# A state space layer: two states in one scan of 512 columns, their start values added to the scan's input

## The chip, the cores and the metric

The kernel runs on one core of a Trainium2 chip. The metric is the device time of one execution in microseconds (us). Before the change it is 8366.49 us, the median of three runs (8362.25 to 8367.0).

A core has five engines that work side by side and wait for one another through semaphores: TensorE (PE in the profile; its weight loads are PEld), VectorE (DVE), ScalarE (ACT), GpSimd (POOL) and SyncE (SP), which starts the transfers here. Each takes its own instructions in program order. SBUF is the large memory on the core, PSUM the small one that TensorE writes to.

## The reference

The program has two layers with a residual each; the change touches only the first. It is a selective state space layer over four images of 64 x 64 positions, taken as L = 4096 tokens. Cut to what matters:

```python
x_dbl = jnp.einsum('bld,ed->ble', xc, x_proj_w)          # xc: 768 channels after a convolution and SiLU
dt = x_dbl[..., :DT_RANK]                                 # 24
Bm = x_dbl[..., DT_RANK:DT_RANK + D_STATE]                # 16
Cm = x_dbl[..., DT_RANK + D_STATE:]                       # 16
dt = jax.nn.softplus(jnp.einsum('blr,dr->bld', dt, dt_w) + dt_b)
A = -jnp.exp(A_log)                                       # 768 x 16

def step(h, inp):
    dt_t, B_t, C_t, x_t = inp
    dA = jnp.exp(dt_t[:, :, None] * A[None])
    dBx = (dt_t * x_t)[:, :, None] * B_t[:, None, :]
    h = dA * h + dBx
    y_t = jnp.einsum('bdn,bn->bd', h, C_t)
    return (h, y_t)

_, ys = jax.lax.scan(step, h0, seq)                       # h0 is zero
y = jnp.moveaxis(ys, 0, 1) + xc * D
y = y * _silu(z)
out = jnp.einsum('bld,cd->blc', y, out_proj_w)
```

Each of the 768 channels has 16 states, and each state is a recurrence along the 4096 tokens: h = dA * h + dBx. The second layer (attention in windows of 7 x 7) comes after the first and is the same in both kernels.

## The kernel before

The 768 channels are six tiles of 128 partitions (ND = 6, index d). The tokens are cut into chunks of T = 256; a chunk of one image is called a step (STEPS = 4 images x 16 chunks = 64, index I). The 16 states of a channel tile are taken in groups of NG = 4 (index g), so a step has M = 24 pairs m = (d, g), each with two halves of two states. A half is a slot: 48 slots in a step. What does not belong to the scans themselves (the projections, the softplus, the output of the step before) is spread over the slots by a plan, and each engine works in the order in which the program emits its instructions.

These are the parts that the change touches. The state's scan needs three inputs: the decay da (ScalarE, into PSUM), the driving term db = dt x B, and the state with which the chunks before ended.

```python
def dt_x(I, d, h):
    h["dtx"][d] = w2.tile([P, T], F32, tag="dtx", name=f"dtx_{I}_{d}")
    nc.gpsimd.tensor_tensor(
        h["dtx"][d], h["dt"][d // 2][:, d % 2, :], h["xc"][d // 2][:, d % 2, :], ALU.mult)

def dt_x_copied(d, h):
    nc.scalar.copy(dtx_ps[:, d % 2, :], h["dtx"][d])           # into PSUM, for VectorE

def driven(I, m, h, eng):                                      # 9 of 24 on GpSimd, 15 on VectorE
    d, g = divmod(m, NS // NG)
    db = w2.tile([P, NG, T], F32, tag="db", name=f"db_{I}_{m}", bufs=6)
    dtx = dtx_ps[:, d % 2, :] if eng is nc.vector else h["dtx"][d]
    eng.tensor_tensor(db, dtx.unsqueeze(1).broadcast_to([P, NG, T]), h["B"][g], ALU.mult)
    dbs[I, m] = db

def decay(I, m, half, h):
    d, g = divmod(m, NS // NG)
    da = ps_a.tile([P, 2, T], F32, tag="da", name="da")        # one PSUM bank, of two
    for k in range(2):
        n = g * NG + 2 * half + k
        act(da[:, k, :], h["dt"][d // 2][:, d % 2, :], AF.Exp, scale=nega[:, d, n : n + 1])
    das[I, m, half] = da

def scans(I, m, half, hs):
    d, g = divmod(m, NS // NG)
    da = das.pop((I, m, half))
    for k in range(2):
        j = 2 * half + k
        n = g * NG + j
        nc.vector.tensor_tensor_scan(
            hs[:, j, :], da[:, k, :], dbs[I, m][:, j, :],
            state[:, d, n : n + 1] if I % NCHUNK else 0.0,
            ALU.mult, ALU.add)

def with_c(I, m, h, hs):
    d, g = divmod(m, NS // NG)
    nc.gpsimd.tensor_copy(state[:, d, g * NG : (g + 1) * NG], hs[:, :, T - 1])
    nc.gpsimd.tensor_tensor(hs, hs, h["C"][g], ALU.mult)

def summed(I, m, h, hs):
    ...                                # TensorE adds the four states' rows up in PSUM (y)
```

The slots in which dt x and the driving terms are made (slot, 1 = on VectorE), and the loop over all m:

```python
driven_at = (
    (-4, 0), (-1, 1), (1, 1), (2, 1), (4, 0), (7, 1), (8, 0), (10, 1),
    (12, 0), (15, 1), (17, 1), (18, 1), (20, 0), (22, 1), (24, 0), (26, 1),
    (26, 1), (26, 1), (30, 0), (33, 1), (36, 0), (39, 1), (40, 0), (43, 1),
)
dt_x_at = (-5, 2, 10, 18, 22, 34)
...
for n in range(STEPS * M):
    I, m = divmod(n, M)
    hs = w2.tile([P, NG, T], F32, tag="hs", name=f"hs_{I}_{m}", bufs=5)
    for half in range(2):
        if 2 * n + half + 1 < len(halves):
            nxt = halves[2 * n + half + 1]
            decay(*nxt, steps[nxt[0]])
        if half == 0:
            if behind:
                with_c(*behind[-1])
            ...                        # summed() of an earlier m
        scans(I, m, half, hs)
        run(I, 2 * m + half, 2 * m + half + 1)     # what the plan has for this slot
    behind.append((I, m, steps[I], hs))
```

A few instructions of the group statistics (once per image) serve as a comparison in the prediction. L251 copies three columns from PSUM, L252 to L254 work on three columns with all operands in SBUF:

```python
def deviation():
    nc.vector.tensor_copy(gm[:, :, 0], t["psmc"][:, 0:NJ])
    nc.vector.tensor_tensor(dev, mv[:, :, 0:1], gm[:, :, 0:1], ALU.subtract)
    nc.vector.tensor_tensor(dev, dev, dev, ALU.mult)
    nc.vector.tensor_tensor(dev, dev, mv[:, :, 1:2], ALU.add)
```

Of the kernel before, what the change touches and what calls it, by code (L numbers as in the profile page):

```python
# [8 lines left out]
F32 = mybir.dt.float32  # L9
# [39 lines left out]
def two_layers(  # L49
# [221 lines left out]
    def layer0(x1s, mvs, gms1):  # L271

        with ExitStack() as es:
            es.enter_context(tc.manual_schedule(engines=in_step))
            ps_a = es.enter_context(tc.tile_pool(name="ps_a", bufs=2, space=PSUM))
# [6 lines left out]
            gms, gbs, st1s = {}, {}, {}  # L282
            dtx_ps = ps_x.tile([P, 2, T], F32, name="dtx_ps")

# [45 lines left out]
            def normed(I, h, at):  # L330
# [10 lines left out]
                def by_group():  # L341
                    h["xn"] = w2.tile([P, NJ, T], F32, tag="xn", name=f"xn_{b}_{i}", bufs=1)
                    for j in range(NJ):
                        act(
                            h["xn"][:, j, :], h["x"][:, j, :], AF.Identity,
                            scale=gms[b][:, j, 1:2], bias=gbs[b][:, j, :],
                        )
# [17 lines left out]

                def root():
                    act(h["var"][:, 0, :], h["var"][:, 0, :], AF.Ln, bias=eps)
                    act(h["var"][:, 0, :], h["var"][:, 0, :], AF.Exp, scale=-0.5)

                at(12, load)  # L370
                at(22, by_group)
                at(24, lambda: mean("xn", "mu"))
                at(26, lambda: with_row("mu", ALU.subtract))
                at(30, square)
                at(31, lambda: mean("sq", "var"))
                at(34, root)
                at(35, lambda: with_row("var", ALU.mult))
# [16 lines left out]
            def with_bias(dst, pb, bias):  # L394

                for k in range(2):
                    act(dst[:, k, :], pb[:, k, :], AF.Identity, bias=bias[:, k : k + 1])

            def prepared(I, h, at):
# [22 lines left out]
                at(-11, kept)  # L422
                for p, (x, c, z) in enumerate((
                    ((-10, -9, -6), (1, 2, 5), (9, 10, 13)),
                    ((-6, -5, -2), (3, 4, 7), (12, 13, 16)),
                    ((-4, -3, 0), (7, 8, 11), (15, 16, 19)),
                )):
                    d = 2 * p
                    pair(("x", p), x, lambda pb, k, d=d: in_proj(pb, k, d + k, h["xn"]))
                    at(x[2], lambda p=p, d=d: with_bias(  # L430
                        xb[:, d : d + 2, KC - 1 :], h["pb"][("x", p)], binp[:, d : d + 2]
                    ))

                    def conv_out(p=p, d=d):
                        c = w2.tile([P, 2, T], F32, tag="xc", name=f"xc_{b}_{i}_{d}", bufs=6)
                        with_bias(c, h["pb"][("c", p)], cvb[:, d : d + 2])
                        h["xc"].append(c)

                    pair(("c", p), c, lambda pb, k, d=d: conv(pb, k, d + k))
                    at(c[2], conv_out)  # L440

                    def z_out(p=p, d=d):
                        z = w2.tile([P, 2, T], F32, tag="sz", name=f"sz_{b}_{i}_{d}", bufs=6)
                        with_bias(z, h["pb"][("z", p)], binp[:, ND + d : ND + d + 2])
                        h["sz"].append(z)

                    pair(("z", p), z, lambda pb, k, d=d: in_proj(pb, k, ND + d + k, h["xn"]))
                    at(z[2], z_out)
# [15 lines left out]
                def rows():  # L464
# [6 lines left out]
                    for tag in "BBBCBCCC":  # L471
                        g = len(h[tag])
                        t = bc.tile([P, NG, T], F32, tag=tag, name=f"{tag}_{b}_{i}_{g}")
                        r0 = g * NG + (NS if tag == "C" else 0)
                        src = rows[r0 : r0 + NG, :]
                        nc.sync.dma_start(t, src.unsqueeze(0).broadcast_to([P, NG, T]))
                        h[tag].append(t)

                at(26, burst)
                at(28, lambda: x_proj((0, 1, 2)))  # L480
                at(29, lambda: x_proj((3, 4, 5)))
                at(32, rows)

                def softplus(q, first):
# [12 lines left out]
                    def parts():  # L497
                        t["e"] = w2.tile([P, 2, T], F32, tag="sp_e", name=f"spe_{b}_{i}_{q}")
                        t["r"] = w2.tile([P, 2, T], F32, tag="sp_r", name=f"spr_{b}_{i}_{q}")
                        for k in range(2):  # L500
                            bias = dtb[:, 2 * q + k : 2 * q + k + 1]
                            act(t["e"][:, k, :], t["pb"][:, k, :], AF.Abs, bias=bias)
                            act(t["r"][:, k, :], t["pb"][:, k, :], AF.Relu, bias=bias)

                    def exped():
                        act(t["e"], t["e"], AF.Exp, scale=-1.0)
                        act(t["pb"], t["e"], AF.Identity, bias=1.0)
# [15 lines left out]
                    at(first, project)  # L523
                    at(first + 3, parts)
                    at(first + 4, exped)
                    at(first + 5, logged)
                    at(first + 6, lost)
                    at(first + 7, added)

                for q, first in enumerate((34, 36, 46)):  # L530
                    softplus(q, first)

            dbs, das = {}, {}
# [21 lines left out]
            def decay(I, m, half, h):  # L555

                d, g = divmod(m, NS // NG)
                da = ps_a.tile([P, 2, T], F32, tag="da", name="da")
                for k in range(2):
                    n = g * NG + 2 * half + k  # L560
                    act(da[:, k, :], h["dt"][d // 2][:, d % 2, :], AF.Exp, scale=nega[:, d, n : n + 1])
                das[I, m, half] = da

            def scans(I, m, half, hs):

                d, g = divmod(m, NS // NG)
                da = das.pop((I, m, half))
                for k in range(2):
                    j = 2 * half + k
                    n = g * NG + j  # L570
                    nc.vector.tensor_tensor_scan(  # L571
                        hs[:, j, :], da[:, k, :], dbs[I, m][:, j, :],
                        state[:, d, n : n + 1] if I % NCHUNK else 0.0,
                        ALU.mult, ALU.add,
                    )

            def with_c(I, m, h, hs):

                d, g = divmod(m, NS // NG)
                nc.gpsimd.tensor_copy(state[:, d, g * NG : (g + 1) * NG], hs[:, :, T - 1])  # L580
                nc.gpsimd.tensor_tensor(hs, hs, h["C"][g], ALU.mult)  # L581
# [18 lines left out]
            def turn(I, p, h, at, s):  # L600
# [26 lines left out]
                at(s, out)  # L627
                at(s + 1, back)
                at(s + 4, gated)

            def out_proj(I, h, at):
# [37 lines left out]
                at(10, reload)  # L669
                for n, slot in enumerate((17, 18, 19, 20, 22, 23)):  # L670
                    m, part = divmod(n, 2)
                    at(slot, lambda m=m, part=part: tile_part(m, range(3 * part, 3 * part + 3)))
                at(26, lambda: residual(0, 2))
                at(28, lambda: residual(2, 1))
                at(30, stats)
# [6 lines left out]
            plan = [[[] for _ in range(SLOTS)] for _ in range(STEPS + 3)]  # L682

            def slot_of(I):
                def at(s, what):
                    plan[I + s // SLOTS][s % SLOTS].append(what)

                return at

            driven_at = (
                (-4, 0), (-1, 1), (1, 1), (2, 1), (4, 0), (7, 1), (8, 0), (10, 1),
                (12, 0), (15, 1), (17, 1), (18, 1), (20, 0), (22, 1), (24, 0), (26, 1),
                (26, 1), (26, 1), (30, 0), (33, 1), (36, 0), (39, 1), (40, 0), (43, 1),
            )
            dt_x_at = (-5, 2, 10, 18, 22, 34)

            for I in range(STEPS):
                h = steps[I]  # L700
                for p in range(ND // 2):
                    turn(I, p, h, slot_of(I), (p + 1) * (SLOTS // 3) + 4)
# [3 lines left out]
                for d, slot in enumerate(dt_x_at):  # L706
                    slot_of(I)(slot, lambda I=I, d=d, h=h: dt_x(I, d, h))
                    slot_of(I)(slot + 2, lambda d=d, h=h: dt_x_copied(d, h))
                for m, (slot, vector) in enumerate(driven_at):
                    eng = nc.vector if vector else nc.gpsimd  # L710
                    slot_of(I)(slot, lambda I=I, m=m, h=h, eng=eng: driven(I, m, h, eng))
# [16 lines left out]
            def run(I, a=0, z=SLOTS):  # L728
                for slot in plan[I][a:z]:
                    for what in slot:  # L730
                        what()

            run(-2)
            run(-1)
            M = ND * NS // NG
            halves = [(I, m, half) for I in range(STEPS) for m in range(M) for half in range(2)]
            decay(*halves[0], steps[0])
            behind = []
            for n in range(STEPS * M):
                I, m = divmod(n, M)  # L740
                hs = w2.tile([P, NG, T], F32, tag="hs", name=f"hs_{I}_{m}", bufs=5)
                for half in range(2):
                    if 2 * n + half + 1 < len(halves):
                        nxt = halves[2 * n + half + 1]
                        decay(*nxt, steps[nxt[0]])
# [419 lines left out]
```

## Time and profile before

| | PE | DVE | ACT | POOL |
|---|---|---|---|---|
| busy us of a span of 8357.8 us | 7252.0 | 7311.7 | 5812.2 | 7092.7 |
| share of the span | 87% | 87% | 70% | 85% |

The profile is that of one execution. A line of its groups names the source line, the engine and operation, what is written and read, the shapes and the count; then the group's busy time in us, the mean duration of one instruction in ns, and the engine's idle time just before these instructions with what ended it. A busy time counts overlapping instructions once, so it can be less than count times mean. In the view of busy tenths the span is cut into 40 slices, and a digit is the busy share of a slice (9 is 90% or more). A timeline's line has the start in us, the length in us, the engine, the line and the operation; neighbours of one kind are merged into one line with a count. L96 is the helper through which ScalarE's activations go.

### The profile page before, as it was taken

What the parts mean: (1) busy time and instruction counts of PE and PEld (TensorE: products, weight loads), DVE (VectorE), ACT (ScalarE), POOL (GpSimd) and SP (SyncE); (2) the same over time, 40 slices, a digit from 0 to 9 for tenths busy, and PEclk for the clock granted to TensorE, in tenths of its full rate; (3) what the DMA queues carried; (4) which work ended last, traced back from release to release, by engine and by line L of the source; (5) the groups of instructions that cost most, each with busy time, mean ns of one, the idle gap of its engine ahead of it and who ended that gap; (6) DMA issues with size and microseconds to landing.
All of it is one profiled execution on the core that took longest, in us unless ns stands there. A gap on an engine that the chain in (4) does not pass through costs nothing. (4 is left out here: it accounts for less than half of the span.)

```text
span 8357.8 us, 139186 instructions
## 1 busy us (share of the span) xinstructions
PE 7252.0 (87%) x45882; PEld 5495.0 (66%) x45882; DVE 7311.7 (87%) x13300; ACT 5812.2 (70%) x13758; POOL 7092.7 (85%) x5719
## 2 busy tenths in 40 slices
PE   7888888888888888888888888888699999999999
PEld 5776677777666677776777677766555555555555
DVE  5999999999999999999999999999856666666666
ACT  5777777777777777777777777777545455455455
POOL 4999999999999999999999999999767677777677
PEclk9998898889889998899898889989799999999999
DMA  3111211121112111211211111112122232232222
GB/s 112 59 61 66 75 58 55 63 74 58 62 66 74 53 58 66 72 58 64 68 63 53 58 65 60 55 57 71 65 89 86 76 94 88 78 92 85 83 87 65
DMA packets 327504, 583.06 MB, mean 70 GB/s; under 512 B 62940, under 2 KB 211180, under 8 KB 326660
## 3 DMA queue, kind: packets, MB, share of 16 engines
q1 hardware_dynamic: 326788, 574.17, 21.3%
q8 instruction: 370, 6.06, 0.3%
q14 instruction: 346, 2.83, 0.1%
HBM read 471.49 MB, written 84.73 MB: 67 GB/s over the span
## 5 line engine op out<-in xcount | busy, mean ns | idle before, releaser
L571 DVE TENSOR_TENSOR_SCAN hs<-da,state,db 128x256 f32<-128x256 f32 x5760 | 3855.0, 728 | 88.9 <-ACT da L96 64.8
L96 ACT ACTIVATE da<-dt,nega 128x256 f32<-128x256 f32 x6144 | 2917.7, 477 | 1208.2 <-DVE hs L571 1100.8
L581 POOL TENSOR_TENSOR hs<-hs,C 128x1024 f32<-128x1024 f32 x1536 | 3621.7, 2358 | 123.9 <-POOL state L580 0.4
L594 PE MATMUL y<-ident,hs 128*128 128x128 f32 x12288 | 1774.6, 296 | 904.5 <-POOL hs L581 902.3
L594 PEld LDWEIGHTS y<-ident,hs 128*128 128x128 f32 x12288 | 1540.5, 153 | 1207.9 <-POOL hs L581 1098.9
L941 POOL TENSOR_SCALAR sg<-sg,rsum 128x308 f32<-128x308 f32 x1536 | 1619.9, 1073 | 633.8 <-DVE rsum L939 631.8
L550 POOL TENSOR_TENSOR db<-dtx,B 128x1024 f32<-128x1024 f32 x576 | 1360.5, 2362 | 0.1
L550 DVE TENSOR_TENSOR db<-dtx_ps,B 128x1024 f32<-128x1024 f32 x960 | 1141.3, 1199 | 0.0
L382 PE MATMUL mm_ps<-xn,w_in 128*128 128x256 f32 x4608 | 1127.4, 392 | 10.1 <-DVE yg L624 8.1
L96 ACT ACTIVATE sg<-sg,mx 128x308 f32<-128x308 f32 x1536 | 828.7, 541 | 251.3 <-DVE mx L926 236.7
L926 DVE CUSTOM_DVE_ANT_0 sg<-lg_ps,bias 128x308 f32<-128x308 f32 x1536 | 643.1, 475 | 375.1 <-PE lg_ps L920 375.1
L382 PEld LDWEIGHTS mm_ps<-xn,w_in 128*128 128x128 f32 x4608 | 872.5, 197 | 119.1 <-DVE yg L624 8.4
L389 PE MATMUL mm_ps<-xb,dcv 128*128 128x256 f32 x3072 | 783.9, 409 | 0.0
L389 PEld LDWEIGHTS mm_ps<-xb,dcv 128*128 128x128 f32 x3072 | 615.7, 208 | 88.3 <-issue 0.3
L969 ACT COPY tb<-pt_ps 88x512 f32<-88x512 f32 x384 | 222.2, 579 | 624.7 <-PE pt_ps L965 624.7
L580 POOL COPY state<-hs 128x4 f32<-128x4 f32 x1536 | 289.1, 188 | 341.8 <-DVE hs L571 328.0
L639 PE MATMUL mm_ps<-yg,w_out 128*128 128x256 f32 x2304 | 539.8, 385 | 0.0
L956 DVE COPY ta<-pt_ps 110x512 f32<-110x512 f32 x768 | 492.4, 682 | 23.2 <-PE pt_ps L951 23.2
L639 PEld LDWEIGHTS mm_ps<-yg,w_out 128*128 128x128 f32 x2304 | 439.6, 195 | 59.1
L951 PE MATMUL pt_ps<-ident,sg 128*110 128x128 f32 x3072 | 417.7, 279 | 0.8 <-POOL sg L941 0.8
L951 PEld LDWEIGHTS pt_ps<-ident,sg 128*110 128x110 f32 x3072 | 322.7, 133 | 77.9 <-issue 47.6
L824 PE MATMUL mm_ps<-xn,w_qkv 128*128 128x512 f32 (+2 forms) x612 | 270.7, 579 | 60.4 <-DVE xn L811 53.2
(141 smaller groups left out, 9152.5 us busy)
## 6 DMA issues: line engine op xcount, KB each, us to landing
B<-bcrows SPq DMA_DIRECT2D x256, 512.0 KB
C<-bcrows SPq DMA_DIRECT2D x256, 512.0 KB
vw<-vd SPq DMA_DIRECT2D x1792, 33.0 KB
xr<-x SPq DMA_DIRECT2D x28, 1056.0 KB
vd<-v SPq DMA_DIRECT2D x280, 96.0 KB
xi<-in_x_dram SPq DMA_DIRECT2D x64, 384.0 KB
xo<-in_x_dram SPq DMA_DIRECT2D x64, 384.0 KB
x<-xo SPq DMA_DIRECT2D x64, 384.0 KB
```

The lines of the kernel that those rows point to most:

```text
L96: ins = nc.scalar.activation(o, i, func, **kw)
L382: nc.tensor.matmul(pb[:, k, :], w_in[:, j, m * P : (m + 1) * P], xn[:, j, :], start=(j == 0), stop=(j == NJ - 1),)
L389: nc.tensor.matmul(pb[:, k, :], dcv[:, d, c, :], xb[:, d, c : c + T], start=(c == 0), stop=(c == KC - 1),)
L550: eng.tensor_tensor(db, dtx.unsqueeze(1).broadcast_to([P, NG, T]), h["B"][g], ALU.mult)
L571: nc.vector.tensor_tensor_scan(hs[:, j, :], da[:, k, :], dbs[I, m][:, j, :], state[:, d, n : n + 1] if I % NCHUNK else 0.0, ALU.mult, ALU.add,
L581: nc.gpsimd.tensor_tensor(hs, hs, h["C"][g], ALU.mult)
L594: nc.tensor.matmul(y[:, d % 2, half, :], hs[:, k, half * P : (half + 1) * P], ident, is_transpose=True, start=(first and half == 0 and d % ...
L639: nc.tensor.matmul(h["po", first][:, m - first, :], w_out[:, d, m * P : (m + 1) * P], h["yg"][d // 2][:, d % 2, :], start=(d == 0), stop=( ...
L926: nc.vector.tensor_tensor_reduce(sg[:, hh, :], lg[:, :NK], bias[:, 4 * m + hh, :], -1.0, BIG, ALU.add, ALU.min, mx[:, hh : hh + 1],)
L941: nc.gpsimd.tensor_scalar(sg[:, hh, :], sg[:, hh, :], rs[:, hh : hh + 1], None, ALU.mult)
L951: nc.tensor.transpose(pt[: KN[c], col : col + P], sg[:, 2 * pair + hh, KOFF[c] : KOFF[c] + KN[c]], ident,)
L956: nc.vector.tensor_copy(t[: KN[0], :, :].rearrange("p a q -> p (a q)"), pt[: KN[0], :])
```

## The change

Two states (a half) are scanned in one instruction of 2 x 256 = 512 columns, with the constant start value 0. For the second state not to take over the end of the first, the decay of the first token of each is held at zero: the two banks of da are set up once with a zero in column 0, and ScalarE writes columns 1 to 255 only. What the first token should have received, its decay times the state before, is added to the first column of db instead. The decay of the first token is e0 = exp(dt[0] * A) for 16 states at once (ScalarE), times the state (VectorE), and then four columns of it are added to each db (VectorE). The first chunk of an image starts from zero and needs none of this.

The copy of the last states goes from GpSimd to ScalarE. ScalarE's work of a slot is now emitted ahead of the other engines' work of that slot, and a pair of activations that shared a slot may be apart; some slots have moved by one. The transfers of B come before those of C. The aim is fewer and longer scans on VectorE and less work on GpSimd.

The core of the diff:

```diff
-            ps_a = es.enter_context(tc.tile_pool(name="ps_a", bufs=2, space=PSUM))
+            ps_a = es.enter_context(tc.tile_pool(name="ps_a", bufs=1, space=PSUM))
 ...
+            AT = {
 ...
+                "start": (-6, -5, -4, -3, 7, 8),
 ...                                   (driven, dtx: as before)
+                "started": (
+                    -2, 0, 2, 3, 7, 8, 11, 11, 15, 16, 18, 19, 23, 23, 27, 27, 27, 28, 35, 34,
+                    39, 40, 43, 44,
+                ),
 ...
+            da_ps = [ps_a.tile([P, 2, T], F32, name=f"da_{half}") for half in range(2)]
+            for t in da_ps:
+                nc.vector.memset(t[:, :, 0:1], 0.0)
 ...
+            def start_decay(d, h):
+                h["e0", d] = w2.tile([P, NS], F32, tag="e0", name=f"e0_{d}", bufs=ND)
+                act(
+                    h["e0", d], nega[:, d, :], AF.Exp, scale=h["dt"][d // 2][:, d % 2, 0:1]
+                )
+            def start_kept(d, h, eng):
+                eng.tensor_tensor(h["e0", d], h["e0", d], state[:, d, :], ALU.mult)
+            def started(I, m, h, eng):
+                d, g = divmod(m, NS // NG)
+                db = dbs[I, m]
+                eng.tensor_tensor(
+                    db[:, :, 0], db[:, :, 0], h["e0", d][:, g * NG : (g + 1) * NG], ALU.add
+                )
 ...
-            def decay(I, m, half, h):
+            def decay(I, m, half, k, h):
 ...
+                act(
+                    da_ps[half][:, k, 1:], h["dt"][d // 2][:, d % 2, 1:], AF.Exp,
+                    scale=nega[:, d, n : n + 1],
+                )
             def scans(I, m, half, hs):
+                pair = slice(2 * half, 2 * half + 2)
+                nc.vector.tensor_tensor_scan(
+                    hs[:, pair, :].rearrange("p k t -> p (k t)"),
+                    da_ps[half].rearrange("p k t -> p (k t)"),
+                    dbs[I, m][:, pair, :].rearrange("p k t -> p (k t)"),
+                    0.0, ALU.mult, ALU.add,
+                )
+            def kept_states(I, m, hs):
 ...
+                nc.scalar.copy(state[:, d, g * NG : (g + 1) * NG], hs[:, :, T - 1])
             def with_c(I, m, h, hs):
-                d, g = divmod(m, NS // NG)
-                nc.gpsimd.tensor_copy(state[:, d, g * NG : (g + 1) * NG], hs[:, :, T - 1])
-                nc.gpsimd.tensor_tensor(hs, hs, h["C"][g], ALU.mult)
+                nc.gpsimd.tensor_tensor(hs, hs, h["C"][m % (NS // NG)], ALU.mult)
 ...
+                    if I % NCHUNK:
+                        at(AT["start"][d], lambda d=d, h=h: start_decay(d, h), ACT)
+                        at(
+                            AT["start"][d] + 1,
+                            lambda d=d, h=h: start_kept(d, h, nc.vector),
+                        )
 ...
+                    if I % NCHUNK:
+                        at(AT["started"][m], lambda I=I, m=m, h=h, eng=nc.vector: started(I, m, h, eng))
 ...
+                    acts, others = plan[I][2 * m + half]
+                    if half == 0 and behind:
+                        acts.insert(0, lambda last=behind[-1]: kept_states(*last[:2], last[3]))
                     if 2 * n + half + 1 < len(halves):
                         nxt = halves[2 * n + half + 1]
-                        decay(*nxt, steps[nxt[0]])
+                        acts.insert(0, lambda nxt=nxt: decay(*nxt, 0, steps[nxt[0]]))
+                        acts.insert(2, lambda nxt=nxt: decay(*nxt, 1, steps[nxt[0]]))
+                    for what in acts:
+                        what()
```

## The prediction

> **What bounds the kernel now.** I read the page first, and of it the busy tenths in slices, because the change touches only the first layer. They split the span: some 29 of 40 slices have VectorE and GpSimd at nine tenths, then both fall. The first part is layer 0 (64 chunks of 256 tokens, "steps" from here on), and only it can move.
>
> ```profile
> DVE  5999999999999999999999999999856666666666
> ACT  5777777777777777777777777777545455455455
> POOL 4999999999999999999999999999767677777677
> ```
>
> Next the busy times by stretch, for one steady millisecond of layer 0 (busy us of PE, PEld, DVE, ACT, POOL, then clock and DMA). VectorE has 983.69 of 1000 us: it is the bound. GpSimd has 919, ScalarE 788.
>
> ```profile
> 2000.00:3000.00 1000.00, 842.42 (x4422) 698.08 (x4421) 983.69 (x1431) 788.05 (x1722) 918.65 (x691) 0.89 0.19 65
> ```
>
> Then the groups of instructions between 2000 and 5000 us, which give the sizes.
>
> ```profile
> L571 DVE TENSOR_TENSOR_SCAN hs<-da,state,db 128x256 f32<-128x256 f32 x2920 | 1954.4, 728 | 44.7 <-ACT da L96 33.2 <-POOL hs L581 7.7
> L581 POOL TENSOR_TENSOR hs<-hs,C 128x1024 f32<-128x1024 f32 x778 | 1834.6, 2358 | 62.7
> ...
> L550 POOL TENSOR_TENSOR db<-dtx,B 128x1024 f32<-128x1024 f32 x292 | 689.9, 2363 | 0.0
> L550 DVE TENSOR_TENSOR db<-dtx_ps,B 128x1024 f32<-128x1024 f32 x486 | 577.7, 1200 | 0.0
> ...
> L580 POOL COPY state<-hs 128x4 f32<-128x4 f32 x778 | 146.6, 188 | 176.5 <-DVE hs L571 168.9 <-PE mm_ps L389 4.2 <-DVE gmean_a L262 1.9
> ...
> L571 DVE TENSOR_TENSOR_SCAN hs<-da,db 128x256 f32<-128x256 f32 x192 | 117.3, 667 | 8.2 <-ACT da L96 6.7 <-issue 1.5
> ...
> L624 DVE TENSOR_TENSOR yg<-mm_ps,sz 128x512 f32<-128x512 f32 x97 | 64.2, 662 | 0.0
> ```
>
> The 2920 + 192 scans at 96 per step make 32.4 steps, so a step takes 92.5 us, and 64 steps take 5920 us. Starts follow one another faster than the mean durations say, since consecutive instructions overlap by about 0.08 us. In the timeline of VectorE four scans start at 2999.66, the next instruction at 3002.25: 0.648 us per scan. That instruction is a 1024-column product, and its successor starts at 3003.36: 1.11 us. So VectorE's step is 96 x 0.648 = 62.2 us of scans, 15 x 1.11 = 16.7 us of products, and the eight groups of other work (417.8 us in 656 instructions, less 656 x 0.08, over 32.4 steps) 11.3 us: 90.2 us, which agrees with 98% of 92.5.
>
> Last I asked the trace for the few VectorE instructions that have the form of the new ones: a few columns, both inputs in SBUF. Those are the group statistics, L252 to L254. First their durations (min/median/max), then VectorE's timeline around one of them, then GpSimd's.
>
> ```profile
> L252 DVE TENSOR_TENSOR dev_b<-mv,gm_b x4: 161/2046/2056, 1761.1 to 6090.3; 128x3 f32<-128x3 f32 x4
> ```
> ```profile
> 1760.88 0.15 DVE L251 COPY gm_b<-psmc_b 128x3 f32<-128x3 f32 x1
> 1761.07 2.05 DVE L252 TENSOR_TENSOR dev_b<-mv,gm_b 128x3 f32<-128x3 f32 x1
> 1763.16 0.16 DVE L253 TENSOR_TENSOR dev_b<-dev_b 128x3 f32<-128x3 f32 x1
> ```
> ```profile
> 1760.75 2.36 POOL L550 TENSOR_TENSOR db<-dtx,B 128x1024 f32<-128x1024 f32 x1
> 1764.88 0.19 POOL L580 COPY state<-hs 128x4 f32<-128x4 f32 x1 [1.78 <-DVE hs L571]
> ```
>
> Three columns take 0.16 us when GpSimd is idle and 2.05 us here. The 2.05 us end at 1763.12, where GpSimd's product ends (1763.11). A copy from PSUM 0.2 us earlier was not held, although the same GpSimd product was running.
>
> [...] The kernel before keeps out of it: its frequent VectorE instructions all have one operand in PSUM (da, dtx_ps, mm_ps). [...] 256 columns of scan take 667 ns from a constant start, 512 columns of product 662 ns.
>
> **The change, part by part.** *Scans.* A scan of 512 columns should cost what 1024 columns of product cost, 1.20 us, or 1.11 to 1.12 us from start to start. A step then has 48 x 1.12 = 53.8 us instead of 62.2: 8.4 us saved, all on the bounding engine. About a third of it is the start value that is no longer fetched (728 against 667 ns).
>
> *New small VectorE work.* In 60 of the 64 steps (not the first of an image) there are 24 additions of four columns (db + e0) and 6 products of 16 columns (e0 x state). Alone each is 0.16 us, and about 0.1 us from start to start (the instruction after L254 starts 0.08 us after it): 3 us. Without any waiting VectorE's step is 90.2 - 8.4 + 3 = 84.8 us.
>
> *GpSimd* loses 24 copies of 0.188 us: 85.0 (91.9% of 92.5) becomes 80.5 us. *ScalarE* takes the 24 copies and 6 exponentials of 16 columns. Its smallest instructions in this trace (32x1) take 0.20 to 0.24 us, so some 6 us on top of 72.9: 79 us. Neither reaches VectorE's sum, and ScalarE can run one scan ahead, since there are still two da banks.
>
> [...] All 30 new instructions have both inputs in SBUF (db and e0, e0 and state), and GpSimd's work in layer 0 all reads SBUF. So each waits for the end of whatever GpSimd is doing, up to 2.36 us. Two estimates of the sum:
>
> First, from the timelines as they are: at the end of each slot in which the change puts such an instruction I took what was left of GpSimd's current instruction, in 55 steps. The rests repeat from step to step almost to 0.02 us (2.1 us at slot 7, 1.8 at 15, 0 at 2 and 3). Summed over the slots it is 26.8 us per step. But GpSimd is 92% busy there, and will be less so in a longer step: times 80.5/108 over 0.92 it is 21.7 us.
>
> Second, a walk by hand through the 48 slots: VectorE's order as in the diff, 1.12 us a scan, 1.11 a product; GpSimd 2.32 us a product and 0.70 a dtx, the product with C starting 0.9 us after the scan it needs, because ScalarE's decay (0.48) and the copy (0.2) now come before it, with 0.1 us for each of two handovers (my choice). Waits come out at slots 0 (2.1 us), 2 (0.6), 7 (0.4), 8 (2.7, two instructions), 11 (0.5), 15 (1.6), 16 (1.1), 18 (0.5), 23 (2.7, two), 27 (1.2), 34 (0.2), 35 (1.1), 39 (1.1), 40 (1.6), 43 (3.7, two) and 46 (2.0); the others find GpSimd idle, often because it waits for VectorE in turn. The sum is 23.1 us, or 0.77 us per instruction.
>
> With 23 us the step is 84.8 + 23 = 107.8 us. VectorE now idles 1.8 us per step; I keep 0.7[...]: 108.5 us. Sixty steps then cost 60 x (108.5 - 92.5) = 960 us more, the four first steps of an image save some 5 us each, and I take about 100 us off because a late VectorE shifts GpSimd into starving more than my walk shows: 8366 + 960 - 20 - 96 = 9210 us.
>
> **The rivals.** [...] The small instructions fall where GpSimd is idle: then the step is 84.8 + 1.8 = 86.6 us, and the time 8366 - 60 x 5.9 - 20 = 7990 us. For it: the rests repeat exactly, so a schedule could be set to miss them, and GpSimd will be idle a quarter of a step. Against it: in the walk eight even slots lie less than a product's length after the start of one, and slots 8, 11, 23, 27, 43 and 46 hold several such instructions back to back.
>
> *ScalarE becomes the wait.* A da bank is now released once per 512 columns, and the states' copy stands between two decays. ScalarE needs 2 x 0.48 us plus the copy and two handovers after each scan, about 1.4 us, against 1.12 us of the other scan, so slots without other VectorE work could lose 0.2 to 0.3 us. At 20 such slots that is 5 us: 91.5 us per step, about 8300 us if it stands alone. It speaks against it that in the lines above only 33 us of VectorE's 3000 are lost to da[...].
>
> *GpSimd always comes first.* [...] each would cost two products, 30 x 1.5 = 45 us: 130 us per step, 10,600 us. Against it: the shown instruction got in at the end of the first product. But the second of a pair met a new one (dev_a: 0.19 us, then 0.65 us behind a dtx), which the walk has in it.
>
> **Range and chances.** Per instruction 0.45 us of waiting gives 13.5 us, a step of 99 us and 8740 us; 1.0 us gives 30 us, 115.5 us and 9730 us. My phases are rough, so the range is nearly that: 8750 to 9650. The waits break even at about 7 us per step (84.8 + 0.7 + 7 = 92.5), and 2% of the time is 167 us, 2.8 us per step. So faster by over 2% needs waits below some 4 us, 0.14 us each, when the mean rest of a product is 1.2 us and GpSimd is busy three quarters of the time: 0.06. Within 2% needs 4 to 10 us: 0.04. Slower: 0.90.
>
> **What would show it.** In the profile after, the scans should be 3072 instructions of about 1.20 us and the step about 108 us. The additions db<-db,e0 (1440 of them) should have a mean near 0.9 us, with a minimum of 0.16 and a maximum near 2.4, ending where GpSimd's instructions end. VectorE stays at nine tenths by waiting inside these instructions; GpSimd falls to about 75%, ScalarE too. It would be wrong if the additions had a mean near 0.2 us (then 7990), if scans of 512 took clearly more than 1.2 us, or if VectorE's idle time before the scans, put down to da, grew to several us per step.

## The result, and the profile after

The changed kernel takes 8965.94 us (median of four runs, 8963.7 to 8969.91) against 8366.36 us: a ratio of 1.0718, 95% interval 1.07 to 1.0737. It is slower by 600 us. The prediction said 9210 us, 8750 to 9650.

First the busy tenths. VectorE is still full through layer 0, GpSimd has fallen, and the layer reaches further into the span: its last scan starts at 6619 us instead of 6020, so the whole loss lies in this layer.

```profile
DVE  6999999999999999999999999999966666666666
ACT  5777777777777777777777777777745545455454
POOL 4878777887778788877777887787757767677677
```

The same steady millisecond as before (busy us of PE, PEld, DVE, ACT, POOL):

```profile
2000.00:3000.00 1000.00, 771.53 (x3989) 627.54 (x3988) 986.53 (x1112) 729.62 (x1848) 797.21 (x393) 0.88 0.18 59
```

VectorE's share is what it was (987 against 984 us), in 1112 instructions instead of 1431. The waits lie inside the durations of its instructions (an addition takes up to 2401 ns, below, and the additions have 0.0 us of idle time before them) and count as busy; so the busy view alone would not show what happened. The groups from 2000 to 5000 us do:

```profile
L635 DVE TENSOR_TENSOR_SCAN hs<-da,db 128x512 f32<-128x512 f32 x1410 | 1681.9, 1208 | 2.7 <-ACT da L96 2.3 <-issue 0.3
L648 POOL TENSOR_TENSOR hs<-hs,C 128x1024 f32<-128x1024 f32 x705 | 1660.7, 2358 | 606.5 <-ACT state L644 573.6 <-DVE e L592 18.7 <-PE y L661 8.4
...
L598 DVE TENSOR_TENSOR db<-db,e 128x4 f32<-128x4 f32 x678 | 407.0, 613 | 0.0
...
L592 DVE TENSOR_TENSOR e<-e,state 128x16 f32<-128x16 f32 x168 | 141.4, 842 | 0.4
...
L644 ACT COPY state<-hs 128x4 f32<-128x4 f32 x704 | 129.7, 184 | 0.0
```

Four columns take 613 ns on the mean, nearly as much as 512 columns of product (662 ns in the kernel before). Over the whole run (min/median/max):

```profile
L598 DVE TENSOR_TENSOR db<-db,e x1440: 128/208/2401, 200.4 to 6616.1; 128x4 f32<-128x4 f32 x180
```

And this is one place, VectorE first, then GpSimd:

```profile
2998.97 3.49 DVE L635 TENSOR_TENSOR_SCAN hs<-da,db 128x512 f32<-128x512 f32 x3
3002.38 1.20 DVE L617 TENSOR_TENSOR db<-dtx_ps,B 128x1024 f32<-128x1024 f32 x1
3003.49 1.21 DVE L635 TENSOR_TENSOR_SCAN hs<-da,db 128x512 f32<-128x512 f32 x1
3004.62 4.40 DVE L598 TENSOR_TENSOR db<-db,e 128x4 f32<-128x4 f32 x2
3008.94 1.21 DVE L635 TENSOR_TENSOR_SCAN hs<-da,db 128x512 f32<-128x512 f32 x1
```
```profile
3004.31 2.37 POOL L648 TENSOR_TENSOR hs<-hs,C 128x1024 f32<-128x1024 f32 x1
3006.64 2.36 POOL L617 TENSOR_TENSOR db<-dtx,B 128x1024 f32<-128x1024 f32 x1
```

The pair of additions ends at 3009.02, the second of two GpSimd products at 3009.00. The first addition waits out the product that is running; by the time it is through, GpSimd has begun the next, and the second addition waits for that one too. Eight columns of addition cost VectorE 4.3 us, which is almost four scans. The ends agree throughout the trace: of the 1800 additions and products 862 take over 250 ns, and each of these ends 18 to 35 ns behind the end of a GpSimd instruction; of the short ones none starts with more than 0.2 us of a GpSimd instruction left. A step, from a slot's scan to the same scan one step on, is 102.4 us in most of layer 0, against 92.5 before.

One thing in the text ahead of the prediction was wrong: it says that ScalarE's work of a slot is emitted ahead of the other engines' work. The code means that, but does the opposite. A slot of the plan is a pair of lists, the first for kind 0 (all but most of ScalarE's work), the second for kind ACT = 1, and the main loop unpacks it as `acts, others`. So what the plan has for TensorE, VectorE and GpSimd in a slot comes before its scan, and what it has for ScalarE after; the decays and the copies of the states stay ahead of the scan. The values are the same either way here, but the phases are not those of the walk in the prediction. An experiment below exchanges the two names.

### The profile page after: what moved, and what is told of

Its sections match the earlier page's. It is cut to its first block, busy times and chain, and to the rows that moved or that the text cites. A ratio compares the mean times of both kernels' runs of the same rounds, so it can differ in the third digit from the quotient of the medians.

```text
span 8964.9 us, 137292 instructions
## 1 busy us (share of the span) xinstructions
PE 7400.6 (83%) x45882; PEld 5518.2 (62%) x45882; DVE 7921.4 (88%) x12030; ACT 5935.8 (66%) x15653; POOL 6852.7 (76%) x4183
## 5 line engine op out<-in xcount | busy, mean ns | idle before, releaser
L96 ACT ACTIVATE da<-dt,nega 128x255 f32<-128x255 f32 x6144 | 2917.4, 477 | 1738.0 <-DVE hs L635 1647.3
L635 DVE TENSOR_TENSOR_SCAN hs<-da,db 128x512 f32<-128x512 f32 x3072 | 3663.3, 1208 | 12.5 <-ACT da L96 12.1
L661 PE MATMUL y<-ident,hs 128*128 128x128 f32 x12288 | 1860.5, 304 | 978.6 <-POOL hs L648 976.4
L661 PEld LDWEIGHTS y<-ident,hs 128*128 128x128 f32 x12288 | 1586.4, 157 | 1353.0 <-POOL hs L648 1241.5
L418 PE MATMUL mm_ps<-xn,w_in 128*128 128x256 f32 x4608 | 1151.6, 395 | 13.8 <-DVE yg L691 11.9
L598 DVE TENSOR_TENSOR db<-db,e 128x4 f32<-128x4 f32 x1440 | 879.4, 624 | 0.0
L425 PEld LDWEIGHTS mm_ps<-xb,dcv 128*128 128x128 f32 x3072 | 644.3, 215 | 102.0 <-issue 0.3
L679 PE MATMUL mm_ps<-ident,ys 128*128 128x128 f32 x768 | 185.6, 331 | 198.1 <-ACT ys L672 197.9
```

The costliest lines, as they stand in the source:

```text
L96: ins = nc.scalar.activation(o, i, func, **kw)
L418: nc.tensor.matmul(pb[:, k, :], w_in[:, j, m * P : (m + 1) * P], xn[:, j, :], start=(j == 0), stop=(j == NJ - 1),)
L425: nc.tensor.matmul(pb[:, k, :], dcv[:, d, c, :], xb[:, d, c : c + T], start=(c == 0), stop=(c == KC - 1),)
L598: eng.tensor_tensor(db[:, :, 0], db[:, :, 0], h["e0", d][:, g * NG : (g + 1) * NG], ALU.add)
L635: nc.vector.tensor_tensor_scan(hs[:, pair, :].rearrange("p k t -> p (k t)"), da_ps[half].rearrange("p k t -> p (k t)"), dbs[I, m][:, pair, ...
L661: nc.tensor.matmul(y[:, d % 2, half, :], hs[:, k, half * P : (half + 1) * P], ident, is_transpose=True, start=(first and half == 0 and d % ...
```

## The experiments

The theory is that each of the 30 small VectorE instructions per step, with both its inputs in SBUF, waits for the end of the GpSimd instruction that is running, as L252 did in the kernel before (2.05 us, and 0.16 us where it did not wait). What in the hardware makes it wait is not shown by any run; the experiments try whether the place of the inputs decides. Where an expectation sets figures without a name against those of a rival, they are this theory's. Rival 1 says that they are slow in themselves (they read back what was just written, with a long stride, or what ScalarE has just copied). Rival 2 says that ScalarE is the cost: its copies hold GpSimd's products back, and a da bank is released once per 512 columns. Rival 3 is the order of the lists.

**e0 in PSUM.** No new PSUM tile is made: a single copy of dtx takes the place of two, which leaves half of the tile dtx_ps for e0, and two slots move for it.

```diff
-                h["e0", d] = w2.tile([P, NS], F32, tag="e0", name=f"e0_{d}", bufs=ND)
+                h["e0", d] = dtx_ps[:, 1, d * NS : (d + 1) * NS]
-                nc.scalar.copy(dtx_ps[:, d % 2, :], h["dtx"][d])      # and where it is read
+                nc.scalar.copy(dtx_ps[:, 0, :], h["dtx"][d])
-                "dtx_ps": (-3, 4, 12, 20, 24, 36),                    # driven: m = 15 at 26
+                "dtx_ps": (-3, 4, 12, 20, 26, 36),                    # driven: m = 15 at 25
```

> The 24 additions and 6 products per step keep their number, engine and shape, but e0 lies in PSUM, in the half bank that a single dtx copy leaves free, so each has one SBUF input only. [...] their means fall from 624 and 842 ns to 130 to 200 ns, none is over 0.4 us, the step falls from 102.4 to 86 to 88 us and the time to 7950 to 8100 us. Rival 1, the small instructions are slow by themselves (a read after a write in db, an input with a long stride, the state that ScalarE has just copied): means stay near 624 and 842 ns, time 8850 to 9000. Rival 2, the loss is ScalarE's (copies and the da bank released once per 512 columns): the instructions get short, but VectorE waits for da instead, time over 8500.

Measured: 8387.8 us, ratio 1.0024 (1.0014 to 1.0033). The additions, over the whole run:

```profile
L598 DVE TENSOR_TENSOR db<-db,dtx_ps x1440: 120/138/166, 202.4 to 6040.0; 128x4 f32<-128x4 f32 x180
```

The columns of db, their stride and the state that ScalarE has copied are the same as before, so rival 1 is out, and the time is under the 8500 us that rival 2 would need. It is still 288 us above the expectation. A part of that is my edit: with the lists as they are, the copy at slot 26 lands behind ScalarE's six SiLU and the table loads on both sides of them (together 5.8 us from 3044.24 us on), and VectorE waited for it once per step, 3.4 us at 3050 us, for instance, and 179 us in the whole run. The run set right, below, is 115 us faster; the other 173 us are not the edit's, so the expectation was too low. Because of the same edit the products of m = 16 and 17 read the dtx of the tile before; the work is the same in amount, but two of 24 products have another tile's values. So this run settles the instructions' duration and not the size of the gain.

**The control**: the same slots and the single copy, e0 left in SBUF (the same two products read the tile before).

> Control for the run before: the same single dtx copy and the same two moved slots (copy of tile 4 at slot 26, one product at 25), but e0 stays in SBUF. All theories: within 1.5% of the changed kernel, 8830 to 9100 us, means of the small instructions about 0.6 and 0.8 us.

Measured: 9044.6 us, ratio 1.0809 (1.0793 to 1.0825).

```profile
L598 DVE TENSOR_TENSOR db<-db,e x1440: 132/207/2398, 207.4 to 6695.5; 128x4 f32<-128x4 f32 x180
```

The moved slots and the single copy alone cost some 80 us. The two kernels differ only in where e0 lies, and the one with e0 in PSUM is 657 us faster.

**The same, set right**: the copy at slot 25, ahead of the burst and behind the product of m = 15.

```diff
-                "dtx_ps": (-3, 4, 12, 20, 26, 36),
+                "dtx_ps": (-3, 4, 12, 20, 25, 36),
```

> e0 in PSUM as in the first run, with the copy of tile 4's dtx at slot 25, ahead of ScalarE's burst of SiLU at 26, and its products after it, so nothing is left out or mixed up. [...] the small instructions take 0.12 to 0.2 us, the step is that without starts (87.7 us, 8097) plus 30 x 0.1 us: 8150 to 8350 us. Rival (slow by themselves, or by ScalarE's handover): over 8700 us.

Measured: 8272.3 us, ratio 0.9886 (0.9871 to 0.9901), a step of 90.6 us. Moving 96 columns of e0 to PSUM takes 694 us off the changed kernel and puts it 1.1% ahead of the kernel before. The additions, over the whole run:

```profile
L598 DVE TENSOR_TENSOR db<-db,dtx_ps x1440: 124/136/166, 202.0 to 5921.2; 128x4 f32<-128x4 f32 x180
```

**The small instructions on GpSimd.**

```diff
-                            lambda d=d, h=h: start_kept(d, h, nc.vector),
+                            lambda d=d, h=h: start_kept(d, h, nc.gpsimd),
-     ... h=h, eng=nc.vector: started(I, m, h, eng)
+     ... h=h, eng=nc.gpsimd: started(I, m, h, eng)
```

> The 30 small instructions go to GpSimd[...]. [...] VectorE's step is 81.7 us, GpSimd's 80.5 + 30 x 0.2 = 86.5 us, so GpSimd bounds with some waiting for its inputs: step 88 to 92 us, time 8100 to 8350 us. Rival 2 (ScalarE): over 8500 us as well as before.

Measured: 8347.4 us, ratio 0.9978 (0.9969 to 0.9986), at the upper end of what was expected. There the same additions take 188/202/252 ns. VectorE now waits for them, 146 us of 3000 before its scans, since they stand in GpSimd's queue behind whole products (2.36 us each).

**Without starts.** Every chunk starts from zero; e0, its products and the additions are left out.

> Leaves out e0, the products and the additions: every chunk starts from zero. What stays of the change is the scan of 512 columns, the copies on ScalarE and the order of the slots. [...] VectorE 81.7 us of work, GpSimd 80.5, step 83 to 86 us, time 7800 to 8000 us, scans 1.21 us each. Rival 2 (ScalarE) or a loss by the new order of the slots: over 8366 us.

Measured: 8097.4 us, ratio 0.9678 (0.9664 to 0.9693), slower than the 8000 us that I had as the upper end. The step is 87.7 us on the mean of the undisturbed ones (87.1 to 88.5) where 83 to 86 were expected. The waits from 2000 to 5000 us (total, times, longest) show why:

```profile
POOL hs L648 <- ACT state L644: 237.6, 178, 4.0
DVE mm_ps L557 <- ACT dt L96: 70.9, 100, 0.9
...
DVE hs L635 <- ACT da L96: 33.4, 83, 0.6
```

VectorE, no longer held in small instructions (they took 20.0 us per step in the changed kernel), waits for ScalarE: 2.1 us per step for the logarithm in the softplus, 1.0 us for da (34 steps in the window). In the changed kernel the same two waits are 38.2 and 2.3 us of 3000: the waiting inside the small instructions covered them. So scans, copies and order of the change gain 269 us, and the starts cost 869 us, together the 600 us of the result.

**Small instructions on tiles of their own.** The kernel without starts, with additions put in at the same slots that nothing waits for:

```diff
+                nc.vector.tensor_tensor(both[:, :n], left[:, :n], right[:, :n], ALU.add)
 ...
+                        at(AT["start"][d] + 1, lambda: apart(NS))
 ...
+                        at(AT["started"][m], lambda: apart(NG))
```

> The run without starts (8097 us, every chunk from zero) with 30 VectorE instructions per step put in at the slots of the products and additions: the same shapes (24 of four columns, 6 of 16), both inputs in SBUF, but on three small tiles of their own that nothing else touches, so no instruction waits for them and they wait for no one's data. [...] they wait for GpSimd's instructions as db and e0 did, mean 0.5 to 0.8 us, 8850 to 9000 us, nearly all of the changed kernel's time. Rival (reading db back, its stride, the state from ScalarE): mean under 0.2 us, 8200 to 8300 us.

Measured: 9124.4 us, ratio 1.09 (1.0882 to 1.0919). They take as long as those that do the work:

```profile
L589 DVE TENSOR_TENSOR both<-left,right x1800: 127/308/2310, 198.6 to 6778.5; 128x4 f32<-128x4 f32 x176, 128x16 f32<-128x16 f32 x4
```

Neither db nor the state nor any data of ScalarE's is involved. It costs more than expected (1027 us over the 8097, where 750 to 900 were expected). The 30 instructions take 733 ns on the mean, 22.0 us per step against 20.0 in the changed kernel, which is 120 us over 60 steps. Why they wait longer is not shown; the additions of the changed kernel also wait for their data, which may shift them against GpSimd.

**The lists exchanged.**

```diff
-                    acts, others = plan[I][2 * m + half]
+                    others, acts = plan[I][2 * m + half]
```

> The changed kernel unpacks the two lists of a slot the wrong way round: in the main loop the work of TensorE, VectorE and GpSimd comes before the scan of the slot, and ScalarE's work after it. Here the two names are exchanged, so ScalarE's work comes first and the rest behind the scan, as the walk by hand in the prediction had it. [...] the 30 small instructions still have both inputs in SBUF and still wait, at other phases: 8700 to 9300 us, and nearer to the walk's 108 us per step than the changed kernel's 102.4. Rival, the exchanged lists are the cause of the loss: under 8500 us.

Measured: 9153.7 us, ratio 1.0939 (1.0923 to 1.0955), a step of 105.3 us; the additions' median is 394 ns instead of 208. The order moves the phases and with them the sum of the waits; the time changes by 190 us here, and the order is not the cause of the loss. In the emitted order that the prediction took for granted, its 108.5 us per step would have been 3% too many.

**Both.**

> Both: e0 in PSUM and the two lists of a slot exchanged. If [...] the exchanged lists cost what VectorE waits for the logarithm of the softplus (some 2 us per step in the run without starts), then 8000 to 8150 us. If the order doesn't matter, 8150 to 8350 us.

Measured: 8229.2 us, ratio 0.9835 (0.9819 to 0.9852), 80 us above the upper end for the case that the exchange saves the wait for the logarithm, and within the range for the case that the order doesn't matter. The copy is back at slot 26, which in this order comes ahead of its products. Exchanging the lists gains 43 us once the additions no longer wait (144 ns on the mean): the wait for the logarithm is gone (62.1 us of 3000 before), but the one for da has grown from 56.7 us:

```profile
DVE hs L635 <- ACT da L96: 82.6, 138, 1.5
```

**The copies of the states back on GpSimd**, first in the changed kernel:

```diff
-                nc.scalar.copy(state[:, d, g * NG : (g + 1) * NG], hs[:, :, T - 1])
+                nc.gpsimd.tensor_copy(state[:, d, g * NG : (g + 1) * NG], hs[:, :, T - 1])
```

> The changed kernel with the copies of the states back on GpSimd. [...] GpSimd is busy for 4.5 us more per step, so the small instructions meet it more often: 8950 to 9200 us. Rival (ScalarE's copies hold GpSimd's products back and that is what costs): under 8850 us.

Measured: 8962.0 us, ratio 1.0709 (1.0693 to 1.0725): the same as the changed kernel. GpSimd's busy time in the steady millisecond rises from 797 to 830 us, and the time doesn't follow. That falls at the bottom of what the theory expected (8950 to 9200 us) and speaks against rival 2. Then in the kernel with e0 in PSUM and the lists exchanged; here both decays also come ahead of all other work of ScalarE's slot.

> e0 in PSUM, lists exchanged, copies of the states on GpSimd as in the kernel before. GpSimd's 80.5 us per step become 85 of about 88: if its wait for ScalarE's copy (303 us in 3000 at present) was in the way, 8080 to 8180 us; if its work is, 8229 to 8300 us.

Measured: 8265.3 us, ratio 0.9876 (0.9861 to 0.9891), 36 us more than with the copies on ScalarE. But the decays have moved too. The next run has the decays as here and the copies on ScalarE behind them, and is 82 us slower than this one; the last run, with ScalarE's copy ahead of them, is 57 us faster. So what handing over the copies is worth depends on where ScalarE makes them, and is at most 1% either way once the additions no longer wait.

**ScalarE's copy behind both decays** of its slot instead of between them (`acts.insert(1, ...)` for the second decay, with e0 in PSUM and the lists exchanged). In the odd slots, which have no copy, the same edit puts the second decay ahead of ScalarE's first other activation.

> e0 in PSUM, lists exchanged (8229 us), and ScalarE copies the states behind both decays of its slot instead of between them. If the 2.5 us per step that VectorE waits for da come from the copy between the decays: 8080 to 8160 us. If not: 8229 within 0.4%, or slower where GpSimd's products, which wait for the copy, become the wait.

Measured: 8346.9 us, ratio 0.9973 (0.9963 to 0.9984): 118 us slower, so my reading of the da wait was wrong. It did not fall but grew, from 82.6 to 118.7 us of 3000, and GpSimd's idle time before its products with C grew from 308 to 358 us. That a later copy delays GpSimd, and GpSimd then VectorE, would fit; it is not shown, since the decays of the odd slots have moved in the same edit. The last run has the copy ahead of both decays.

> e0 in PSUM, lists exchanged (8229 us), and ScalarE's copy of the states ahead of both decays of its slot. Behind both it cost 118 us more, by holding GpSimd's products back. If GpSimd's wait for the copy is what is left, going first gains a part of that: 8100 to 8200 us. If VectorE's wait for da takes its place (the decays come 0.2 us later, and it already waits 2.5 us per step for them): 8200 to 8280 us.

Measured: 8208.7 us, ratio 0.9811 (0.9798 to 0.9825), a step of 89.6 us. It gains 20 us and lies in the second of the two ranges; VectorE's wait for da is still 76.3 us of 3000. It is the fastest of the kernels here that compute the whole layer (the run without starts is faster), and 158 us ahead of the kernel before.

## Why the prediction was right, and where it was off

*The bound and the cause.* Right. VectorE is at 98% in both kernels, and the additions have a minimum and a maximum near those predicted (0.128 and 2.40 us, where 0.16 and 2.4 were named), the long ones all ending where GpSimd's instructions end; only their mean is 0.62 us instead of 0.9. The proof is the pair of runs with e0 in PSUM or in SBUF and nothing else different (8388 against 9045 us), and the additions on tiles of their own. Without the waits the 30 instructions cost 2.9 us per step (8272 us with e0 in PSUM against 8097 without starts, over 60 steps), where 3 us were predicted.

*The scans.* Predicted 1.20 us, measured 1.208. In the timeline the next instruction starts 3.41 us after the first of three: 1.137 from start to start against 1.12 assumed, so 54.6 us per step instead of 53.8. One statement of the prediction about them is wrong: that about a third of the 8.4 us saved comes from the constant start. From its own figures (728 against 667 ns, 96 scans) it is 5.9 us, about 70%.

*The waits: the mis-sized term.* The prediction put the waits at 23.1 us per step. The 24 additions (624 ns on the mean over the whole run) and the 6 products (844 ns) take 15.0 + 5.1 = 20.0 us per step. Less 30 x 0.16 us alone that leaves 15.2 us. That is 7.9 us per step less than predicted. The scans (0.8 us more) and the idle time (0.9 us more) make up for a part, so that the step is 102.4 us instead of 108.5, some 370 us over 60 steps. Another part was luck: the prediction took 96 us off because GpSimd would starve more than in the walk; in the steady millisecond GpSimd idles 20%, where 80.5 us of work in a step of 108 us would leave 25%. 244 us remain. The cause was right and only this size was off.

*Why it was off.* The walk set each small instruction behind the scan of its slot, and the code sets it before. With the lists exchanged the instructions take 23.0 us per step, that is 18.2 us of waiting, 3 us more than in the changed kernel and still 5 us less than the walk. So the order explains about 40% of the miss. The rest is the walk's own, and the trace of the exchanged run, slot by slot, shows where it lies. In the slots that hold one small instruction the walk has 10.3 us in all and the run 10.4, though single entries differ by up to 1.4 us. In the seven slots that hold two or three (8, 11, 23, 27, 43, 44, 46) the walk has 12.8 us and the run 7.8: 2.7 against 1.6 us for the pair at slot 23, 3.7 against 1.3 us at slot 43. There an instruction right behind a waiting one seldom waited again: 22 of 296 did. The first estimate, the rests read off the timelines of the kernel before, scaled for a less busy GpSimd, gave 21.7 us: little better.

*Idle time.* Right in direction: the waits inside the small instructions hide others. Without starts VectorE idles 4.4% (956 us busy in the mean of three millisecond windows) of 87.7 us, 3.9 us, and in the changed kernel 1.5% of 102.4 us, 1.6 us. But that is hardly less than the 1.8 us of the kernel before, where the prediction had it fall to 0.7.

*The rivals.* That the small instructions fall where GpSimd is idle put the kernel at 7990 us. About half of the additions do slip through (their median is 208 ns), but the other half pay. "ScalarE becomes the wait" is not what costs here (2.3 us of 3000 before the scans), but it is the bound that comes next: the two waits read off the kernel without starts, 3.1 us of its step, are more than the 1.7 us by which that step misses 86. "GpSimd always comes first" is not what happens: a waiting instruction gets in at the end of one GpSimd instruction (18 to 35 ns behind it in the changed kernel). Only the next one right behind it can lose again, and of 120 such in the changed kernel 60 did. What stays open is how much of the 2.3 to 2.5 us that VectorE waits for da in the fastest kernels a better order on ScalarE could take away; two orders were tried.

## What to carry to other kernels

Before moving a few columns of work to VectorE, look at where its inputs lie, not at its size: with both in SBUF, beside a GpSimd that was busy for 80% of the time, an instruction of 0.13 us cost 0.6 us here on the mean and up to 2.4 us, and with one input in PSUM it took 0.14 us. The trace of the kernel before can show that in three or four instructions of the same form; ask for their minimum and maximum (161 and 2056 ns here), since the wait sits inside the duration and no idle time shows it. When a plan by slots is changed, read the emitted order and not its names.

## What the runs showed of the hardware that was not expected

A waiting VectorE instruction got in at the end of one GpSimd instruction (18 to 35 ns behind it, 862 cases), and where a second one stood right behind it, that one waited once more in 60 of 120 cases: the pair in the timeline takes 4.40 us, GpSimd's two products 4.69 us. These 60 are all at this place of the step; the 60 others, all at slot 11, took about 0.15 us, although GpSimd began its next product there too, within 22 ns. What decides between two starts so close is not shown. And the waits came without the same data or tiles too: additions on tiles of their own have a maximum of 2310 ns. A scan that starts from a constant was shorter by 61 ns than one that starts from a column of the state (667 against 728 ns for 256 columns), which is 5.9 us of 96 scans per step; that part of the gain could be had without any addition only if no start were needed.
